# Loads in order of use, column scores ahead of the second tile's first layer, and matmuls that nothing reads, in a two-layer perceiver kernel

## The chip, the cores and the metric

The kernel runs on one core of a Trainium2 chip. A core has five engines that run beside each other, each in its own program order: TensorE (PE: matmuls, with weight loads shown as PEld), VectorE (DVE), ScalarE (ACT), GpSimd (POOL) and SyncE (SP, which here only issues transfers). Transfers run on 16 DMA engines. The metric is the device time of one execution in microseconds, as the median of several runs.

## What is computed

The reference adds six blocks to a stream x of 32 batches with 64 rows of 256 numbers each; a context of 32 batches with 1601 rows of 256 numbers is read by two of them.

```python
x = x + _L0_xattn_ref(_layernorm(x), ctx_1024, W, b)        # [x, mean of the context] @ W.T + b
x = x + _L0_attn_ref(_layernorm(x), ..., slopes)            # 16 heads over the 64 rows, with a slope by distance
x = x + _L0_ffn_ref(_layernorm(x), ...)                     # shared gated MLP, and 2 of 8 routed experts
x = x + _L1_xattn_ref(_layernorm(x), ctx_1024, ...)         # 16 heads of x over the 1601 context rows
x = x + _L1_attn_ref(_layernorm(x), ...)                    # causal convolution, gated recurrence, gated MLP
x = x + _L1_ffn_ref(_layernorm(x), w1, w2)                  # MLP with ternary weights and quantised rows
```

The order matters for what follows: a row of x goes through layer 0 (the first three lines) before its query exists, the query is needed for every score against the context, and layer 1's rest (the last two lines) comes behind that attention.

## The kernel before

**Tiles.** Two batches make a tile of 128 rows, 16 tiles in all. They are taken in the order 1, 2, ..., 15, 0 (`order`), so "pos 0" is the first tile taken and "pos 15" the last. All of it is float32, but for the ternary weights of the last MLP and some small bfloat16 helpers.

**The full stage.** Most of the time goes to the attention over the context. Each tile is cut into `NU` = 13 units (12 pieces of 512 context rows for one half of the heads of one batch, and one unit for the last 65 rows). The loop over `g` (13 x 16 units) does for each unit: `column_scores` (scores with the context on the partitions, L765 and L771, and their exponentials), `values` four units ahead, `row_scores` five units ahead (scores with the rows on the partitions, L723, from which VectorE takes the maxima, L730), `weighted` (the sums over the context, L795) and `keys` six units ahead. The maxima of a half of a tile must be known before its column scores: `maxima` splits their negative into three bfloat16 parts (L736 to L741), `maxima_rows` transposes these, and `column_scores` puts them into the score buffer first.

**The small chains.** Everything else of a tile is a generator that yields wherever it waits for another engine: `layer0` (a layer norm, the mixing with the context mean (`xat`), a second norm, the attention over 64 rows (`k`, `q`, `v`, `s`, a softmax on VectorE and ScalarE, the transposes `tpp`, the head sums `o`, the output `wo`), a third norm and the gated MLP (`su`, `sv`, `th`, the gate `lg`, `so`)); `query` (a norm `d`, a transpose `tp_d`, `q`, and `qbd` on VectorE); `tail` for the last two blocks, which is `recurrent` (norm `e`, transposes `tp_e`, `tp_f`, `tp_g`, the matmuls `pw`, `hg`, `gru`, `ff`, `ffo`) and then `bit_ffn` (the quantising helper `quantised` with its transposes `tpq`, and the matmuls `h`). `Steps` objects in a list `plan` advance these generators at two places of each unit, by due times in sixteenths of a tile. The four compute engines run in the order in which the code is recorded (`manual_schedule`); the order of SP's transfers is set by the framework from priorities and dependencies.

**Before the full stage.** `first` runs layer 0 and the query of pos 0 with nothing else to hide behind, and with it go keys and values of the first pieces (`early`), `early_sums` (context means of pos 1 to 3: four pieces each through the single buffer `part`, loaded by SP at L95 and summed by ScalarE at L243) and, as `beside`, layer 0 of pos 1. Then five row score groups, and what is left of `beside` is run to its end (`beside.all()`) before unit 0.

**The end.** After the last unit `tail` of pos 14 and `tail` of pos 15 are advanced in turn, the latter alone at the end.

**Buffers.** PSUM has three small buffers (`mm_tile`), two of two banks each for scores (`sc_tile`) and one for the weighted sums. A new tile in a buffer waits until the tile before in it has been read. Weights are loaded by `load_w` (L159), from POOL's queue where no engine is named; the rest of layer 1's weights follow from POOL too (L1027 to L1044).

## Time and profile before

| what | time |
|---|---|
| runs before (three) | 2213.13, 2213.56, 2221.24 us; median 2213.56 |
| the profiled execution | 2218.25 us, of which its span is 2216.6 |
| granted TensorE clock, mean over the span | 0.969 |
| PE busy | 2077.8 us (94%) |
| DVE busy | 1342.1 us (61%) |
| ACT busy | 909.1 us (41%) |
| POOL busy | 330.2 us (15%) |

"Span" is the time from the first to the last instruction of the profiled execution. The granted clock is the share of its full speed that TensorE was given; 0.50 in a stretch means that matmuls take twice as long there. In a timeline a line has the start, the duration, the engine, the line of the kernel, the operation, what it writes and reads, the shape and the count; what stands in square brackets is how long the engine had been idle before it and what ended that. In a table by stretches the columns are the stretch, its length, then for PE, PEld, DVE, ACT and POOL the busy time and the number of instructions, the granted clock, the busy share of the DMA engines and the GB/s that they moved.

### The profile page before, as it was taken

To read this page: it belongs to the slowest core of one execution; us is meant where nothing else is said; L and a number is where in the kernel's file an instruction comes from. 1 tells how busy PE (TensorE), PEld (TensorE's weight loads), DVE (VectorE), ACT (ScalarE), POOL (GpSimd) and SP (SyncE) were. 2 spreads that over 40 slices of the span, in tenths; PEclk is the share of its full clock that TensorE was granted. 3 is DMA by queue.
4 is the path that set the end of the run, shared out by engine and by line. 5 is a ranking of instruction groups with operands and counts; after the bars stand their busy time and mean duration, and the time that the engine had idled before them with its cause. 6 is when DMAs were issued, how large, how long until landed. Compare 5 with 4: busy or idle time off the path is not lost. (4 is left out here: it accounts for less than half of the span.)

```text
span 2216.6 us, 69786 instructions
## 1 busy us (share of the span) xinstructions
PE 2077.8 (94%) x31887; PEld 1520.4 (69%) x31903; DVE 1342.1 (61%) x2686; ACT 909.1 (41%) x1397; POOL 330.2 (15%) x545
## 2 busy tenths in 40 slices
PE   5799999999999999999999999999999899999984
PEld 3476777767676777777777677777776566676763
DVE  3446756665656666665666656565667656656554
ACT  3334444444535354444444435353433233334342
POOL 4211211111111121112111111111100000000011
PEclk8699999999999999999999999999999899999996
DMA  7423211111112121111211111110100200011000
GB/s 235 134 92 108 71 64 64 36 65 64 66 61 69 61 66 34 64 66 63 67 64 55 72 34 69 61 37 32 44 34 4 72 32 23 16 41 34 2 5 5
DMA packets 43463, 126.41 MB, mean 57 GB/s; under 512 B 11922, under 2 KB 25250, under 8 KB 43168
## 3 DMA queue, kind: packets, MB, share of 16 engines
q1 hardware_dynamic: 41312, 117.16, 15.8%
q8 instruction: 250, 4.10, 0.8%
q0 software_dynamic: 1296, 3.97, 0.5%
q10 hardware_dynamic: 560, 0.81, 0.1%
q14 instruction: 45, 0.37, 0.1%
HBM read 119.83 MB, written 2.10 MB: 55 GB/s over the span
## 5 line engine op out<-in xcount | busy, mean ns | idle before, releaser
L777 ACT ACTIVATE pt<-s 128x1024 f32<-128x1024 f32 (+1 forms) x416 | 403.5, 1022 | 299.0 <-PE s L771 298.9
L730 DVE TENSOR_REDUCE mx<-r 128x2 f32<-128x1024 f32 x384 | 452.1, 1220 | 114.8 <-PE r L723 114.5
L231 PE MATMUL vps<-w_L_xattn_WvT,ctxT 128*128 128x128 f32 x3072 | 398.9, 284 | 0.0
L231 PE MATMUL kps<-ctxT,w_L_xattn_WkT 128*128 128x512 f32 x768 | 383.9, 623 | 10.4 <-DMA ctxT<-ctxT 10.4
L690 ACT ACTIVATE kt<-kps,chv 128x512 f32<-128x512 f32 x192 | 132.2, 689 | 634.1 <-PE kps L231 634.1
L707 DVE COPY vau<-vps 128x512 f32<-128x512 f32 (+1 forms) x208 | 143.3, 689 | 390.3 <-PE vps L231 390.3
L231 PEld LDWEIGHTS vps<-w_L_xattn_WvT,ctxT 128*128 128x128 f32 x3072 | 362.7, 194 | 23.8 <-issue 3.1
L795 PEld LDWEIGHTS o<-pt,vau 128*32 128x32 f32 (+1 forms) x13312 | 196.5, 110 | 150.1 <-issue 143.3
L795 PE MATMUL o<-pt,vau 128*32 128x64 f32 (+1 forms) x13312 | 231.1, 221 | 4.2 <-ACT pt L777 4.2
L723 PE MATMUL r<-kt,qbd 32*128 32x512 f32 x1536 | 226.2, 649 | 1.4 <-DVE mx L727 0.8
L231 PEld LDWEIGHTS kps<-ctxT,w_L_xattn_WkT 128*128 128x128 f32 x768 | 131.7, 191 | 122.4 <-issue 105.3
L771 PEld LDWEIGHTS s<-qbd,kt 32*128 32x128 f32 x6144 | 207.2, 188 | 3.2
L771 PE MATMUL s<-qbd,kt 32*128 32x128 f32 x6144 | 207.7, 271 | 0.0
L243 ACT ACTIVATE part<-part 128x1601 f32<-128x1601 f32 x60 | 92.7, 1545 | 9.9 <-DMA part<-ctxT 9.6
L723 PEld LDWEIGHTS r<-kt,qbd 32*128 32x128 f32 x1536 | 62.9, 184 | 36.0 <-issue 18.4
L765 PEld LDWEIGHTS <-onesb 3*128 3x128 bf16 x768 | 21.0, 91 | 94.8 <-issue 93.5
L765 PE MATMUL s<-neg,onesb 3*128 3x512 bf16 x768 | 79.6, 386 | 6.9 <-DVE mx L730 6.7
L813 DVE RECIPROCAL rs<-sums 128x128 f32<-128x128 f32 x64 | 60.7, 948 | 1.7 <-PE sums L810 1.7
L309 POOL TENSOR_TENSOR kbd<-kT,mask 128x512 f32<-128x512 f32 x32 | 32.9, 1050 | 137.6 <-ACT kT L302 137.6
L231 PE MATMUL ff<-nT,w_fg 128*128 128x128 f32 x384 | 51.6, 287 | 1.0 <-ACT nT L925 1.0
L231 PEld LDWEIGHTS ff<-nT,w_fg 128*128 128x128 f32 x384 | 47.8, 200 | 1.9 <-ACT nT L925 1.7
L231 PE MATMUL ff<-nT,w_fv 128*128 128x128 f32 x384 | 48.3, 276 | 0.0
(352 smaller groups left out, 2562.7 us busy)
## 6 DMA issues: line engine op xcount, KB each, us to landing
ctxT<-ctxT SPq DMA_DIRECT2D x32, 1601.0 KB, 6.8
part<-ctxT SPq DMA_DIRECT2D x60, 800.5 KB, 4.5
rest<-ctxT SPq DMA_DIRECT2D x32, 65.0 KB, 2.2
x<-x SPq DMA_DIRECT2D x16, 128.0 KB, 2.2
out<-x SPq DMA_DIRECT2D x16, 128.0 KB, 1.7
w<-w SPq DMA_DIRECT2D x16, 128.0 KB, 2.4
sum_L_ffn_w1T<-L_ffn_w1T SPq DMA_DIRECT2D x4, 256.0 KB, 4.3
raw_L_ffn_w1T<-L_ffn_w1T SPq DMA_DIRECT2D x4, 256.0 KB, 3.1
```

The source lines that it names most:

```text
L231: nc.tensor.matmul(o, lhsT=lhsT(c), rhs=rhs(c), start=(c == 0), stop=(c == 1))
L243: nc.scalar.activation(junk, src, AF.Copy, accum_out=csum[:, c, b:b + 1])
L309: nc.gpsimd.tensor_tensor(kbd[oc], kT[:, oc, :].rearrange("p (b k) -> p b k", b=2).unsqueeze(2).to_broadcast([P, 2, 4, S]), mask4.unsqueez ...
L690: nc.scalar.activation(kt, o, AF.Identity, bias=chv[:, hf.oc, BK2:BK2 + 1])
L707: nc.vector.tensor_copy(v[:kr, :, 0:VW - 16].rearrange("p k (h d) -> p k h d", d=17)[:, :, :, 0:16], o[:kr].rearrange("p k (h d) -> p k h ...
L723: nc.tensor.matmul(o, lhsT=qbd[r, q % 2, q // 2].rearrange("p h q -> p (h q)"), rhs=w.kt[r, q, :] if h is None else halves[h].kt[k][r, :], ...
L730: nc.vector.tensor_reduce(w.mx[:, 2 * m:2 * m + 2, h % 4, k], ps[m], AX.X, ALU.max)
L765: nc.tensor.matmul(o, lhsT=onesb[r, :], rhs=halves[h].neg[r, :].unsqueeze(1).to_broadcast([3, 4, P]), start=True, stop=False)
L771: nc.tensor.matmul(ps[i // 2][:kr, i % 2, j * P:(j + 1) * P], lhsT=w.kt[r, j, :] if h is None else halves[h].kt[k][r, j * P:(j + 1) * P], ...
L777: nc.scalar.activation(pt[:kr].rearrange("p i k c -> p i (k c)"), ps[m][:kr], AF.Exp)
L795: nc.tensor.matmul(w.o[32 * c:32 * c + 32, q, m, :], lhsT=v[:kr, j, 17 * hd:17 * hd + 32], rhs=pts[m][:kr, c // 2, j, c % 2 * S:c % 2 * S ...
L813: nc.vector.reciprocal(rs, t)
```

## The change

It has three parts.

*Loads.* x of the first tile is loaded second, before the context (`early_x`). `load_w` uses SP's queue by default. The weights of the mixing stand ahead of the second context piece, the last 65 rows behind it; the other weights of layer 0 follow on SP. The weights of layer 1 that came from POOL are issued on SP by `late_weights`, at the step at which the context sums of pos 1 are complete in the program.

*Order.* Of the two calls of `others()` beside each row score group one goes, and `beside.all()` goes: what is left of pos 1's layer 0 is put into the plan for units 0 to 3. The query of pos 1 is due from 4 instead of 1, the ternary weights from 5 to 23 instead of 0 to 21.

*Matmuls that nothing reads.* `warm(n)` takes a score buffer and records n bfloat16 matmuls (128x128 by 128x512) into it; no instruction reads the result. It is called in `layer0` and `query` of the first tile (5, 22, 11, 6 and 11), before each of the first four row score groups (5 each), and in `recurrent` and `quantised` of the last tile (11, 18, 11, 18 and 18).

```diff
     def load_w(name, cols, chunks=2, eng=None):
-        (eng or nc.gpsimd).dma_start(t, a[name].rearrange("(c p) o -> p c o", p=P))
+        (eng or nc.sync).dma_start(t, a[name].rearrange("(c p) o -> p c o", p=P))
...
+    early_x = {}
+
+    def warm(n):
+        t = sc_tile("warm")
+        for _ in range(n):
+            nc.tensor.matmul(t[:, 0, :], lhsT=identb, rhs=onesb.unsqueeze(1).to_broadcast([P, 4, P]),
+                             start=True, stop=True)
...
-        x = load_x(ti)
+        x = early_x.pop(ti) if ti in early_x else load_x(ti)
...
+        if soon:
+            warm(5)
         xT = transposed(xn, f"b{ti}", SECOND["xT"] if k else "xT")
...
         def weights(oc):
+            if soon and oc == 0:
+                warm(22)
...
+        if soon:
+            warm(11)
         xT = transposed(xn, f"c{ti}", SECOND["xT"] if k else "xT")
...
+        if soon:
+            warm(6)
         o = mm_tile([P, D], f"so_{ti}")
...
-    def query(pos, x):
+    def query(pos, x, soon=False):
...
+        if soon:
+            warm(11)
         xT = transposed(xn, f"d{ti}", "xTq")
...
-    def recurrent(ti, x):
+    def recurrent(ti, x, soon):
...
+        if soon:
+            warm(11)
         t = transposed_ps(xs, f"f{ti}")
...
+        if soon:
+            warm(18)
         o = mm_tile([P, D], f"gru_{ti}")
...
+        if soon:
+            warm(11)
         t = transposed_ps(xs, f"g{ti}")
...
-    def quantised(v, n, tmp, sw, name):
+    def quantised(v, n, tmp, sw, name, soon):
...
+        if soon:
+            warm(18)
         t = mm_tile([P, 8, P], f"tpq_{name}", BF16)
...
-    w_k2 = load_w("L1_xattn_WkT", D, eng=nc.sync)
+    w_k2 = load_w("L1_xattn_WkT", D)
+    early_x[order[0]] = load_x(order[0])
     load_batch(0)
+    w_v2 = load_w("L1_xattn_WvT", D, eng=nc.scalar)
+    w_xat = load_w("L0_xattn_WT", D, 4)
+    load_batch(1)
     wholes[0].rest = load_rest(order[0])
-    w_v2 = load_w("L1_xattn_WvT", D, eng=nc.scalar)
-    load_batch(1)
-    w_xat = load_w("L0_xattn_WT", D, 4, nc.sync)
...
+    def late_weights():
+        for j in range(4):
+            nc.sync.dma_start(w_o2[32 * j:32 * j + 16], ...)
+            nc.sync.dma_start(bv2[32 * j:32 * j + 16], a["bv2"][j])
+        nc.sync.dma_start(w_pw, ...)
+        nc.sync.dma_start(w_hg, ...)
+        nc.sync.dma_start(w_go[:DI], ...)
+        for w, name in ((w_fg, "L1_attn_w_gate"), (w_fv, "L1_attn_w_value")):
+            nc.sync.dma_start(w[:, :, :FF], a[name].rearrange("(c p) f -> p c f", p=P))
+        nc.sync.dma_start(w_fo[:, 0:NF - 1, :], ...)
+        nc.sync.dma_start(w_fo[0:FF - last, NF - 1, :], ...)
...
     def second_layer(pos):
-        yield from tail(order[pos], x4[pos])
+        yield from tail(order[pos], x4[pos], pos == NT - 1)
...
         if pos < NT - 1:
-            planned(queried(pos), 16 * (pos - 1) + 1, 16 * (pos - 1) + 8.5, 6, 0)
+            planned(queried(pos), 16 * (pos - 1) + (1 if pos > 1 else 4), 16 * (pos - 1) + 8.5, 6, 0)
...
+        late = [late_weights]
         while 0 not in queries:
             if early:
                 early.pop(0)()
             ahead.step()
             others()
-        for f in early:
+            if 1 in csums and late:
+                late.pop()()
+        for f in early + late:
             f()
         for g in range(4):
+            warm(5)
             row_scores(g)
             others()
-            others()
         maxima(0)
         row_scores(4)
         others()
         maxima_rows(0)
-        beside.all()
+        if beside.gen is not None:
+            plan.insert(0, Steps(beside.gen, 0, 3, 30 - beside.done, 2))
...
-        planned(all_ternary(), 0, 21, 24, 2)
+        planned(all_ternary(), 5, 23, 24, 2)
```

More of the change, by code (lines that the diff above doesn't have):

```diff
@@ L968, in quantised, with bit_ffn @@
         return qT, d
-    def bit_ffn(ti, x):
+    def bit_ffn(ti, x, soon):
         m = moments(x, f"h{ti}")
@@ L974, in bit_ffn @@
         tmp = work_tile([P, D], "xs", f"qt_{ti}")
-        qT, d = yield from quantised(n, D, tmp, sw1, f"h{ti}")
+        qT, d = yield from quantised(n, D, tmp, sw1, f"h{ti}", soon)
         yield ACT
@@ L982, in bit_ffn @@
         yield
-        qT, d = yield from quantised(h, HID, h, sw2, f"i{ti}")
+        qT, d = yield from quantised(h, HID, h, sw2, f"i{ti}", soon)
         yield
@@ L990, in bit_ffn, with tail @@
         nc.sync.dma_start(out[ti * P:(ti + 1) * P, :], x6)
-    def tail(ti, x):
-        x = yield from recurrent(ti, x)
-        yield from bit_ffn(ti, x)
+    def tail(ti, x, soon):
+        x = yield from recurrent(ti, x, soon)
+        yield from bit_ffn(ti, x, soon)
     order = list(range(1, NT)) + [0]
@@ L1005, in load_batch @@
         ctxs[n] = load_ctx(2 * hf.ti + hf.b)
-    w_k2 = load_w("L1_xattn_WkT", D, eng=nc.sync)
+    w_k2 = load_w("L1_xattn_WkT", D)
+    early_x[order[0]] = load_x(order[0])
     load_batch(0)
+    w_v2 = load_w("L1_xattn_WvT", D, eng=nc.scalar)
+    w_xat = load_w("L0_xattn_WT", D, 4)
+    load_batch(1)
     wholes[0].rest = load_rest(order[0])
-    w_v2 = load_w("L1_xattn_WvT", D, eng=nc.scalar)
-    load_batch(1)
-    w_xat = load_w("L0_xattn_WT", D, 4, nc.sync)
-    w_k = load_w("L0_attn_WkT", D, eng=nc.sync)
-    w_q = load_w("L0_attn_WqT", D, eng=nc.sync)
-    w_v = load_w("L0_attn_WvT", D, eng=nc.sync)
-    w_o = load_w("L0_attn_WoT", D, eng=nc.sync)
-    w_gate = load_w("L0_ffn_w_gateT", E)
+    w_k = load_w("L0_attn_WkT", D)
+    w_q = load_w("L0_attn_WqT", D)
+    w_v = load_w("L0_attn_WvT", D)
+    w_o = load_w("L0_attn_WoT", D)
     w_s1 = load_w("L0_ffn_sw1T", D)
     w_s3 = load_w("L0_ffn_sw3T", D)
+    w_gate = load_w("L0_ffn_w_gateT", E)
     w_s2 = load_w("L0_ffn_sw2T", D)
@@ L1026, in perceiver_kernel @@
     nc.gpsimd.memset(bv2, 0.0)
-    for j in range(4):
-        nc.gpsimd.dma_start(w_o2[32 * j:32 * j + 16], a["L1_xattn_WoT"].rearrange("(g j d) o -> j d g o", j=4, d=16)[j])
-        nc.gpsimd.dma_start(bv2[32 * j:32 * j + 16], a["bv2"][j])
-    w_pw = load_w("L1_attn_pw_wT", D)
+    w_pw = const.tile([P, 2, D], F32, name="w_pw")
     w_hg = const.tile([P, 2, 2 * DI], F32, name="w_hg")
-    nc.gpsimd.dma_start(w_hg, a["L1_attn_w_hg"].rearrange("(c h) d e -> (h d) c e", c=2))
     w_go = const.tile([P, 4, 64], F32, name="w_go")
     nc.gpsimd.memset(w_go[DI:], 0.0)
-    nc.gpsimd.dma_start(w_go[:DI], a["L1_attn_w_out"].rearrange("h e o -> e h o"))
     w_fg = const.tile([P, 2, NF * P], F32, name="w_fg")
     w_fv = const.tile([P, 2, NF * P], F32, name="w_fv")
-    for w, name in ((w_fg, "L1_attn_w_gate"), (w_fv, "L1_attn_w_value")):
+    for w in (w_fg, w_fv):
         nc.gpsimd.memset(w[:, :, FF:], 0.0)
-        nc.gpsimd.dma_start(w[:, :, :FF], a[name].rearrange("(c p) f -> p c f", p=P))
     w_fo = const.tile([P, NF, D], F32, name="w_fo")
     nc.gpsimd.memset(w_fo[:, NF - 1, :], 0.0)
-    nc.gpsimd.dma_start(w_fo[:, 0:NF - 1, :], a["L1_attn_w_ff_out"][0:(NF - 1) * P, :].rearrange("(f p) o -> p f o", p=P))
-    nc.gpsimd.dma_start(w_fo[0:FF - (NF - 1) * P, NF - 1, :], a["L1_attn_w_ff_out"][(NF - 1) * P:FF, :])
+    def late_weights():
+        for j in range(4):
+            nc.sync.dma_start(w_o2[32 * j:32 * j + 16],
+                              a["L1_xattn_WoT"].rearrange("(g j d) o -> j d g o", j=4, d=16)[j])
+            nc.sync.dma_start(bv2[32 * j:32 * j + 16], a["bv2"][j])
+        nc.sync.dma_start(w_pw, a["L1_attn_pw_wT"].rearrange("(c p) o -> p c o", p=P))
+        nc.sync.dma_start(w_hg, a["L1_attn_w_hg"].rearrange("(c h) d e -> (h d) c e", c=2))
+        nc.sync.dma_start(w_go[:DI], a["L1_attn_w_out"].rearrange("h e o -> e h o"))
+        for w, name in ((w_fg, "L1_attn_w_gate"), (w_fv, "L1_attn_w_value")):
+            nc.sync.dma_start(w[:, :, :FF], a[name].rearrange("(c p) f -> p c f", p=P))
+        last = (NF - 1) * P
+        nc.sync.dma_start(w_fo[:, 0:NF - 1, :], a["L1_attn_w_ff_out"][0:last, :].rearrange("(f p) o -> p f o", p=P))
+        nc.sync.dma_start(w_fo[0:FF - last, NF - 1, :], a["L1_attn_w_ff_out"][last:FF, :])
     def ternary(name, chunks, cols):
@@ L1168, in first @@
         x3[0] = yield from steps
-        yield from query(0, x3[0])
+        yield from query(0, x3[0], True)
     def biased():
```

## The prediction

> **What bounds it now.** I read the page's slices first, then busy time in three stages, then the timeline of the first 120 us and of the last 60.

> ```profile
> PE   5799999999999999999999999999999899999984
> PEclk8699999999999999999999999999999899999996
> ```
> ```profile
> 0.00:118.50 118.50, 75.08 (x431) 51.82 (x432) 47.25 (x95) 35.72 (x60) 36.05 (x72) 0.74 0.54 174
> 118.50:2120.00 2001.50, 1945.73 (x30713) 1424.04 (x30726) 1248.45 (x2485) 845.20 (x1284) 278.37 (x445) 0.99 0.16 53
> 2120.00:2216.60 96.60, 56.95 (x751) 44.53 (x751) 46.40 (x107) 28.17 (x53) 15.83 (x28) 0.77 0.02 5
> ```
> The second row's PE is busy 97% at clock 0.99: what the change puts into that stage costs its full TensorE time. All that can be won lies in the first and third rows (clock 0.74 and 0.77), where one tile's chain runs from engine to engine. The first stage in order:

> ```profile
> 28.04 0.43 DVE L187 BATCH_NORM_STATS2 st_a<-x 128x6 f32<-128x256 f32 x1 [17.28 <-DMA x<-x]
> ...
> 34.55 1.40 PE L280 MATMUL xat<-w_L_xattn_WT,xT_a 128*128 128x256 f32 x4
> ...
> 66.53 0.36 ACT L235 ACTIVATE th<-su 128x256 f32<-128x256 f32 x1
> ...
> 84.59 1.12 DVE L662 SCALAR_TENSOR_TENSOR qbd<-q,chv,mask2q 128x128 f32<-128x128 f32 x4 [2.57 <-PE q L231]
> ...
> 118.49 0.61 PE L765 MATMUL s<-neg,onesb 3*128 3x512 bf16 x4
> ```
> The first tile's x arrives only at 28.0; its queries (qbd) are done at 85.7; the first column scores start at 118.49. The clock, microsecond by microsecond:

> ```profile
> 76.00:77.00 1.00, 0.61 (x2) 0.29 (x2) 0.85 (x3) 0.00 (x0) 0.21 (x2) 0.62 0.62 256
> ...
> 83.00:84.00 1.00, 1.00 (x13) 0.83 (x10) 0.00 (x0) 0.99 (x3) 0.00 (x0) 0.96 0.00 0
> ```
> It falls to half at about 76.2, 2.0 us after a matmul group ended at 74.2, and returns at 83.0, 5.4 us after TensorE became busy again at 77.6. Elsewhere: it fell 4.4 us after 47.9, 3.1 us after 2162.1; it rose 4.6 us after 30.7, 4 us after 2184.8, and only 8.5 us after 64.35. So waits of 2 to 4.4 us lose it; 4 to 8.5 us of work bring it back.

> **The change, part by part.** *Price of one idle matmul.* The nearest rows are the 128x512 bf16 matmuls of the last MLP: three in 0.81 us at full clock (each 0.38 long, so one starts every 0.215) and two in 1.06 at half clock (0.63 long, one every 0.43). A group of 11 is 2.4 or 4.7 us, 18 is 3.9 or 7.7.

> *First loads.* x now stands second on SP's queue, ahead of the first context piece: 0.13 MB at the 346 GB/s of 10:20 put that piece, and the keys that wait for it at 10.4, 0.4 us later. The second piece (landed 20.5, 2.81 + 17.7) gets w_xat ahead of it (0.52 MB, 1.5 us), but POOL's weights, 1.4 MB by then, are out of its way (4 us): about 18, and no sum waits for it. POOL loses its transfers; its fills end near 8 and its next work is behind x's statistics, so that is worth nothing. In the built program each SP transfer waits for the one eight places earlier; that binds only the small weights behind the second piece, whose first reader (k) comes at 32. With x there, the next wait is the column sums: ScalarE's second sum ended at 22.2 (20.61 + 1.54), set by the keys before it, and mT can follow at 22.5 instead of 34.51: 12.0 earlier. Two blocks of values (2.0 each) and five idle matmuls (1.1) now stand ahead of tp_b, which moves from 40.2 to about 30.1. The softmax wait of 5.8 us before tpp takes 22 idle matmuls (4.7) without delay; at full clock tpp, wo and tp_c save 1.0 + 1.0 + 0.3, so xT_c comes at 51.5 instead of 63.9.

> What is late next: ScalarE sums the next tiles' context pieces in program order, and the fifth sum stands ahead of th. There is one "part" buffer: the piece is issued when the last is summed, lands 4.5 us later (median of 60), is summed in 1.74, with 0.15 for the issue: 6.4. Five from 22.4 are 54.4; the third also waits 2.1 for the two exponentials ahead of it: 56.5. So th stands at 57.0, not at 53: **-9.5**. The late weights (2.9 MB, formerly POOL's queue) now lie between those pieces on SP; I leave the landing at 4.5, since DMA was busy 24% in 50:60, but see the second rival.

> *th to qbd.* 18.1 us before. lg needs the buffer that th reads, so TensorE waits 3.0 (54.4 to 57.4) and I take the clock as lost (2.0 lost it above). It returns near the end of xat; then xat saves 0.5, k, q and v run at 1.05 + 1.06 + 1.09 instead of 2.08 + 1.70 + 1.73: 2.8 in all with the rounding of the rise. The 6 idle matmuls lie beside VectorE's chain from xat to tp_b (3.1), the 11 ahead of tp_d have no cover, since tp_d followed q at once: 2.4 lost. Sum about **-0.9**: qbd ends at 75.3.

> *First column scores ahead of the second tile.* From the end of qbd to column scores the trace has 32.8. What stays is VectorE's: 1.29 for s, 1.31, 1.21, four times 2.36, 1.47, 1.05 of maxima, 0.2, together 16.0; ahead of it s_2 and one idle group on TensorE (2.2, beside the 1.29). The idle tile also takes one of the two score buffers, so a row group now waits for both reductions of the last one instead of the first: 0.7 in three places; half-clock row groups cost 1.05 instead of 0.5 each. I take 21 (20 to 24): **-11.8**; column scores at 96.3.

> The rest of the second tile then runs inside units 0 to 2 of the full stage. At full-clock rows: tpp 1.04, o 0.86, wo 1.08, tp_c 0.4, su and sv 2.1, lg 0.5, so 1.03: 7.0. TensorE keeps program order, so three waits stand in front of the row scores and weighted sums queued behind them: pT between the two o groups (1.0 to 1.4), wo to tp_c (60.53 to 63.20: 2.7), the buffer of tp_a (0.3). The clock is half at the start, for 3 to 5 us against 1.1 before: 1.7. Sum **+13.0** (11 to 16). Query and ternary steps that move by units add no TensorE work: 0, bounds -2 to +2 by the 2.5 us of VectorE waits at 180 to 183.

> *The last tile.*

> ```profile
> 2166.19 0.39 PE L965 MATMUL tpq_h<-identb,q_h 128*128 128x128 bf16 x2 [4.06 <-POOL q_h L960]
> ...
> 2168.73 0.64 PE L215 MATMUL tp_f<-ident,xs_f 128*128 128x128 f32 x2
> ...
> 2178.56 1.89 PE L987 MATMUL h<-wq_L_ffn_w2T,qT_i 128*128 128x256 bf16 x8 [1.16 <-DVE zz L904]
> 2180.24 1.81 PE L912 MATMUL gru<-w_go,rr 128*128 128x64 f32 x8
> ```
> In the built order the first 11 stand between h and tp_f, and 18 between h and gru. Neither has a wait there: tp_f and gru follow the work of the tile before at once. Both meet a half clock (waits of 4.06 and 4.36 just before). I take 3.9 (2.4 to 4.7) and 5.6 (3.9 to 7.7). hg gives back 0.9, gru 0.8, tp_g 0.25, ff 1.6 (4.63 to 3.0). The groups of 11 and 18 after that fit the waits of 2.8, 4.9 and 5.3, and the last MLP at full clock saves 0.1 + 0.65 + 0.4 + 0.85. So 9.5 - 5.5 = **+4.0** (+1 to +7).

> **Sum.** -9.5 - 0.9 - 11.8 + 13.0 + 4.0 = -5.2 on the profiled execution (2218.25, span 2216.6). The median of the runs shown is 4.7 lower, 2213.56; from there 2208.4.

> [...]

> **Rivals.** *The clock holds.* If it survives the 3.0 us before lg, lg, xat and so run full: qbd 3 us earlier still; the row groups take 20, units 0 to 2 cost 11, the tail 2.5: -12.4 - 12.8 + 11 + 2.5 = -11.7, 2202. For: at 83.0 to 87.9 it survived waits of 0.7 and 0.8. Against: 76.2. Chance 0.22.

> *Pieces land late, and it is slower.* ScalarE's in-order sums wait for SP's queue, where weights now stand ahead of each piece. The first piece before, behind such weights, took 9.2 (issued 23.06, awaited until 32.4 at most). At 9.2 for all five, th is at 22.4 + 5 x 11.1 = 77.9, 21 later than forecast: 2229. The gain is gone when they land in (5.2 + 2.1)/5 = 1.5 more than 4.5: from 6 us it isn't faster. For: 2.9 MB in 30 us. Against: those weights are issued while the piece before is still being summed. Chance 0.13.

> *The idle matmuls don't lift the clock.* Then the tail pays 4.7 + 7.7 and overruns of 1.9, 2.8 and 2.4: +19.5; the row phase is 24, qbd gains 6.4, units cost 13.5: -6.4 - 8.8 + 13.5 + 19.5 = +17.8, 2231. Against: 2189.0, where dense work did lift it. Chance 0.05.

> **Numbers.** Forecast 0.60, 2208.4, own range 2203 to 2214. A measurement of this kernel can tell about 0.5% from no change: below 2202.5 or above 2224.6. Faster: four fifths of the first rival and a twelfth of the forecast, 0.22. Slower: two fifths of the second and most of the third, 0.08. The rest 0.70. The range 2199 to 2217 leaves out about 0.06 below and 0.12 above.

> **What would show it.** x's statistics near 5 us; th near 57 with a ScalarE wait for "part" ahead of it; qbd near 74, column scores near 96; TensorE waits before tp_c in unit 1; gru 4 us or more after the end of h, where it followed h at once; the last MLP's 128x512 matmuls 0.215 apart. Wrong if th follows xT_c without a wait, if units 0 to 2 show no TensorE waits, or if the tail is shorter than 96 us.

## The result, and the profile after

| | median | lowest to highest | runs |
|---|---|---|---|
| before | 2217.84 us | 2213.13 to 2221.24 | 6 |
| after | 2208.02 us | 2206.75 to 2214.36 | 6 |

The ratio of after to before is 0.9967, with a 95% interval of 0.9952 to 0.9982: a gain of 0.33%, some 7.3 us (4.0 to 10.6); the two medians lie 9.8 apart. The profiled execution after took 2207.64 us, its span 2205.9, 10.7 less than the span before.

The slices of the page after, PE's busy tenths and the granted clock, each digit a fortieth of the span:

```profile
PE   7799999999999999999999999999999899999976
PEclk9999999999999999999999999999999899999998
```

Only the first two digits and the last ones differ from before. The table by stretches of the kernel after (columns as before: PE, PEld, DVE, ACT, POOL, clock, DMA share, GB/s):

```profile
0.00:118.50 118.50, 88.01 (x737) 55.13 (x738) 55.83 (x104) 39.83 (x65) 24.59 (x55) 0.94 0.54 181
118.50:2120.00 2001.50, 1943.01 (x30819) 1424.30 (x30835) 1248.40 (x2493) 849.34 (x1296) 278.05 (x447) 0.99 0.15 52
2120.00:2205.90 85.90, 59.17 (x496) 39.95 (x490) 39.18 (x91) 18.09 (x37) 12.70 (x24) 0.88 0.01 4
```

In the first stretch the clock went from 0.74 to 0.94 and PE is busy 13 us more, with idle matmuls and with the first units, which begin in it now. The middle is what it was. The first stage in the timeline of after:

```profile
5.83 0.43 DVE L197 BATCH_NORM_STATS2 st_a<-x 128x6 f32<-128x256 f32 x1 [1.71 <-DMA x<-x]
...
24.64 1.03 PE L290 MATMUL xat<-w_L_xattn_WT,xT_a 128*128 128x256 f32 x4
...
56.35 1.54 ACT L253 ACTIVATE part<-part 128x1601 f32<-128x1601 f32 x1 [1.85 <-DMA part<-ctxT]
...
57.88 0.36 ACT L245 ACTIVATE th<-su 128x256 f32<-128x256 f32 x1
...
58.56 0.61 PE L241 MATMUL lg<-w_L_ffn_w_gateT,xT_c 128*128 128x8 f32 x4 [1.75 <-ACT xT_a L231]
...
72.22 1.13 DVE L682 SCALAR_TENSOR_TENSOR qbd<-q,chv,mask2q 128x128 f32<-128x128 f32 x4 [4.10 <-PE q L241]
...
95.33 0.62 PE L785 MATMUL s<-neg,onesb 3*128 3x512 bf16 x4 [2.09 <-DVE neg L768]
...
106.73 0.43 PE L397 MATMUL o<-pT,vbd 128*32 128x64 f32 x16 [0.96 <-ACT pT L390]
...
113.93 0.41 PE L225 MATMUL tp_c<-ident,xn_c 128*128 128x128 f32 x2 [2.70 <-DVE xn_c L207]
```

x is there 22 us sooner, xat starts 9.9 sooner, and the chain then meets the context pieces: th stands behind a piece that ScalarE awaits 1.85 us. qbd is 12.4 and the column scores are 23.2 earlier. The same column scores of unit 3 start at 130.68 instead of 143.49, only 12.8 earlier: the rest of the second tile's layer 0 lies in units 0 to 2 now, with two waits of TensorE, 0.96 ahead of o and 2.70 ahead of tp_c. The last tile:

```profile
2155.85 3.45 PE L190 MATMUL warm<-onesb,identb 128*128 128x512 bf16 x11
2159.14 0.38 PE L225 MATMUL tp_f<-ident,xs_f 128*128 128x128 f32 x2
...
2167.75 1.89 PE L1015 MATMUL h<-wq_L_ffn_w2T,qT_i 128*128 128x256 bf16 x8 [1.16 <-ACT qT_i L995]
2169.43 5.00 PE L190 MATMUL warm<-onesb,identb 128*128 128x512 bf16 x18
2174.27 1.00 PE L936 MATMUL gru<-w_go,rr 128*128 128x64 f32 x8
```

tp_f and gru show no wait: each followed at once on idle matmuls, which stood in the queue where before the transpose and gru themselves stood.

### The profile page after: what moved, and what is told of

Read it like the earlier page. It is cut to its first block, busy times and chain, and to the rows that moved or that the text cites. A ratio compares the mean times of both kernels' runs of the same rounds, so it can differ in the third digit from the quotient of the medians.

```text
span 2205.9 us, 70071 instructions
## 1 busy us (share of the span) xinstructions
PE 2090.2 (95%) x32038; PEld 1519.4 (69%) x32054; DVE 1343.4 (61%) x2686; ACT 907.3 (41%) x1397; POOL 315.3 (14%) x525
## 5 line engine op out<-in xcount | busy, mean ns | idle before, releaser
L253 ACT ACTIVATE part<-part 128x1601 f32<-128x1601 f32 x60 | 92.6, 1544 | 17.5 <-DMA part<-ctxT 17.3
L241 PE MATMUL ff<-nT,w_fv 128*128 128x128 f32 x384 | 49.4, 280 | 0.0
```

The lines of the kernel that those rows point to most:

```text
L241: nc.tensor.matmul(o, lhsT=lhsT(c), rhs=rhs(c), start=(c == 0), stop=(c == 1))
L253: nc.scalar.activation(junk, src, AF.Copy, accum_out=csum[:, c, b:b + 1])
```

## The experiments

Each kernel was run beside the kernel before, whose medians there were 2216.02 to 2218.30; the ratio is to that. Dates come from one profiled execution each, which for "order only" and "without the 11 before tp_d" was the slowest of that kernel's runs; the columns th, column scores and unit 3 are starts as well; the last column is from the start of the last `pw` to the end of the span.

| kernel | median, us | ratio (95%) | th | qbd starts | column scores | unit 3 | last pw to the end |
|---|---|---|---|---|---|---|---|
| before | 2217.84 | 1 | 66.53 | 84.59 | 118.49 | 143.49 | 55.5 |
| after | 2208.02 | 0.9967 (0.9952 to 0.9982) | 57.88 | 72.22 | 95.33 | 130.68 | 57.5 |
| no idle matmuls | 2209.17 | 0.9963 (0.9948 to 0.9977) | 56.22 | 74.35 | 94.41 | 131.97 | 55.5 |
| loads only | 2209.98 | 0.9974 (0.9964 to 0.9984) | 57.70 | 73.69 | 104.96 | 131.03 | 55.5 |
| order only | 2214.33 | 0.9990 (0.9978 to 1.0001) | 67.09 | 85.23 | 106.50 | 144.93 | 55.6 |
| late weights on POOL | 2216.85 | 1.0001 (0.9993 to 1.0010) | 64.15 | 78.48 | 101.60 | 139.29 | 57.3 |
| sums first | 2208.02 | 0.9962 (0.9949 to 0.9975) | 55.29 | 69.63 | 92.75 | 128.00 | 57.5 |
| without the 11 before tp_d | 2211.06 | 0.9970 (0.9960 to 0.9981) | 57.50 | 69.47 | 93.05 | 130.58 | 59.1 |
| row groups' in the mm ring | 2209.77 | 0.9965 (0.9952 to 0.9979) | 57.84 | 72.18 | 92.87 | 130.93 | 57.5 |
| spread over units 0 to 5 | 2212.20 | 0.9976 (0.9966 to 0.9986) | 57.34 | 71.68 | 94.80 | 128.20 | 58.6 |
| tail without two groups | 2203.98 | 0.9948 (0.9933 to 0.9963) | 57.33 | 71.68 | 94.79 | 133.00 | 52.7 |
| tail covered | 2201.49 | 0.9939 (0.9922 to 0.9956) | 57.58 | 71.93 | 95.05 | 130.22 | 51.3 |
| combined | 2201.22 | 0.9927 (0.9914 to 0.9941) | 55.25 | 70.94 | 91.62 | 129.52 | 49.4 |
| last | 2196.85 | 0.9903 (0.9886 to 0.9919) | 53.97 | 66.36 | 86.74 | 124.30 | 53.2 |

### The three parts alone

**No idle matmuls**, loads and order as changed:

```diff
     def warm(n):
-        t = sc_tile("warm")
-        for _ in range(n):
...
+        return
```

> The changed kernel without any of its idle matmuls; loads and order stay. My account (the loads carry the gain, the idle matmuls about pay for themselves): th 58 to 60.5 instead of 57.9, since tpp, wo and tp_c run at half clock again; row reductions 3.06 apart instead of 3.75, since the idle tile no longer takes a score buffer; from pw to the end of the span 55.5, as before the change, instead of 57.5; in all 2205 to 2209, the changed kernel's time within 2. Rival (the idle matmuls are what lifts the clock and carry the gain): no clock in the row phase and the tail, 8 to 12 us lost, about 2217.

The time is that of after: all 14 groups together are worth nothing that can be measured. The trace shows gains and losses that about cancel: without them th to qbd takes 18.1 instead of 14.3, but qbd to the column scores 20.1 instead of 23.1, and the tail 55.5 instead of 57.5. Two lines of VectorE's timeline without them:

```profile
78.92 2.35 DVE L746 TENSOR_REDUCE mx<-r 128x2 f32<-128x1024 f32 x2
82.32 2.36 DVE L746 TENSOR_REDUCE mx<-r 128x2 f32<-128x1024 f32 x2 [1.05 <-PE r L739]
```

The reductions are 3.40 apart, not 3.06 as expected: row groups at half clock (the eight matmuls at 87.00 took 3.21, as those of before at 91.64 with the clock at 0.50) leave a gap of 1.05. With the idle matmuls they are 3.75 apart. That th came earlier without them (56.22) was not expected either: the first context piece was issued 1.35 us sooner there (22.89 instead of 24.24), and th stands behind the fifth.

**Loads only**: as above, and the order of before (both calls of `others()`, `beside.all()`, the old due times).

> The first loads of the changed kernel, with the order of steps and the absence of idle matmuls of the kernel before. My account (the loads are the gain, the order gives nothing net): th 58 to 60.5, qbd ends at 76 to 78, the first column scores 32.8 later, 109 to 111, that is 8 to 10 ahead of before, and this lead is kept: 2208 to 2210. Rival (the order carries the gain; the second tile's layer 0 eats an early start): column scores at 115 or later, 2215 to 2218.

The time is as expected. The column scores came 4 sooner than expected, and the lead over before at unit 3, 12.5, is almost that of after (12.8); at the last pw 8.4 are left of it.

**Order only**, on the kernel before:

```diff
             row_scores(g)
             others()
-            others()
...
-        beside.all()
+        if beside.gen is not None:
+            plan.insert(0, Steps(beside.gen, 0, 3, 30 - beside.done, 2))
...
-        planned(all_ternary(), 0, 21, 24, 2)
+        planned(all_ternary(), 5, 23, 24, 2)
```

> The kernel before with only the order of steps changed (column scores ahead of the rest of the second tile's layer 0, query and ternary steps moved). My account: the 10.8 that the changed kernel gains from qbd to the column scores come back as 10.3 in units 0 to 2, so 2216 to 2218, no change. Rival (the order is the gain): 5 or more faster, 2213 or less.

PE's first matmuls of the column scores, units 0 to 3:

```profile
106.50 0.61 PE L765 MATMUL s<-neg,onesb 3*128 3x512 bf16 x4 [2.09 <-DVE neg L748]
118.45 0.39 PE L765 MATMUL s<-neg,onesb 3*128 3x512 bf16 x4
134.94 0.40 PE L765 MATMUL s<-neg,onesb 3*128 3x512 bf16 x4
144.93 0.40 PE L765 MATMUL s<-neg,onesb 3*128 3x512 bf16 x4
```

The first comes 12.0 earlier than before, the fourth 1.4 later: what the order wins it gives back. The median, 2214.33, lies 1.7 below the range of my account; the interval of the ratio, 0.9978 to 1.0001, leaves room for a gain of up to 4.9 us, just short of the rival's 5.

### Which of the loads

**Late weights on POOL's queue**, at the start, as before the change; x stays early:

```diff
-            nc.sync.dma_start(w_o2[32 * j:32 * j + 16],
+            nc.gpsimd.dma_start(w_o2[32 * j:32 * j + 16],
...
+    late_weights()
...
-        late = [late_weights]
+        late = []
```

> The changed kernel with the late weights issued on POOL's queue at the start, as before the change, instead of on SP's between the context pieces. My account (they cost each piece 0.5 to 0.9 of its landing, and the fifth piece 1.8 of ScalarE's wait ahead of th): pieces land in 4.5 instead of 4.9 to 5.3, th at 56.2, where the chain through su holds it, instead of 57.9; the second whole context piece lands later (its sum at 18 to 21 instead of 16.96), which may move mT by up to 2 and eat that. Rival (pieces land late whatever shares the queue): th at 57.5 or later.

My account was wrong, and by more than its rival's bound: the whole gain in the median is gone (1.0001). ScalarE's timeline, then one line of VectorE's:

```profile
26.04 0.37 ACT L231 COPY xT_a<-tp_a 128x256 f32<-128x256 f32 x1 [1.29 <-PE tp_a L225]
36.76 1.54 ACT L253 ACTIVATE part<-part 128x1601 f32<-128x1601 f32 x1 [10.36 <-DMA part<-ctxT]
```
```profile
21.41 0.82 DVE L207 TENSOR_SCALAR xn_a<-x,mv_a,rstd_a 128x256 f32<-128x256 f32 x1 [13.55 <-POOL rstd_a L202]
```

The first piece, issued at 27.70, landed 9.06 later, with DMA at 356 GB/s from 20 to 30; in after it was issued at 24.24 and took 4.94, with DMA at 187 GB/s. So its sum started 7.6 later, and th 6.3 later. The second piece landed in 4.80 again.

A second effect stood in neither account. POOL issued the late weights from 7.78 to 20.40, ahead of rstd_a in its program order. VectorE waited 13.55 us for rstd_a, both context sums ran from 22.14 (in after they started at 11.48 and 16.96), and mT came at 26.43, 2.2 later. That chain doesn't set th here: ScalarE still awaits the fifth piece, for 0.95, just ahead of it.

So what counts in the first loads is that layer 1's weights aren't issued before the first sums are done (from 25.1 in after). With x early and those weights where they were, the trace is 4.2 ahead of before at unit 3, the last tile then takes 1.8 more, and the median gains nothing. The converse, the weights moved and x left where it was, was not run.

**Sums first**: the sums of each whole piece are recorded as soon as it has landed, ahead of the keys' copies.

```diff
+        for _ in range(3):
+            next(steps)
+        both(0)
+        yield
+        both(1)
+        csums[0] = csum
...
-        for b in range(2):
-            yield
-            summed(order[0], csum, b, 0, ctxs[b][:, 0, :], junk)
```

> The changed kernel with the first tile's context sums emitted as soon as each piece lands (ScalarE: ahead of the first keys copy and of the second), so that mT no longer waits for the keys. My account (th is set by five context pieces in a row from the end of the first sums, and by a chain that starts at mT): mT at 18.8 to 19.5 instead of 24.24, th at 52.5 to 53.5 instead of 57.9, column scores at 90 to 91, all of it kept: 4 to 5 faster. Rival (the pieces then compete with the second whole context piece and the weights, and land late): th at 56 or later, no gain.

```profile
18.53 0.29 DVE L284 TENSOR_SCALAR mT<-csum 128x256 f32<-128x256 f32 x1
```
```profile
25.86 1.54 ACT L253 ACTIVATE part<-part 128x1601 f32<-128x1601 f32 x1 [6.13 <-DMA part<-ctxT]
...
53.75 1.54 ACT L253 ACTIVATE part<-part 128x1601 f32<-128x1601 f32 x1 [1.44 <-DMA part<-ctxT]
55.29 0.36 ACT L245 ACTIVATE th<-su 128x256 f32<-128x256 f32 x1
```

mT (VectorE's line) came 5.7 earlier, th (ScalarE's) only 2.6: the first piece, issued at 18.72, took 7.14 to land instead of 4.94, which is part of the rival's account. Neither account had th right (52.5 to 53.5, or 56 and later). th still follows the fifth piece. The 2.6 reach unit 3 (128.00), but the time is that of after; with runs from 2203.5 to 2215.8 a gain of this size can't be told.

### Idle matmuls without cover, in the first stage

**Without the 11 before tp_d:**

```diff
-        if soon:
-            warm(11)
         xT = transposed(xn, f"d{ti}", "xTq")
```

> The changed kernel without the 11 idle matmuls ahead of tp_d alone. My account (they have no cover and the clock is already full there): tp_d follows q at 67.5, qbd starts at 70.0 instead of 72.2, and th to qbd's start shrinks from 14.3 to 12.1; column scores 2 earlier. Rival (they are what carries the clock over the waits to qbd and the first row groups): th to qbd stays at 14 or the row phase from qbd grows from 23.1 to 25.

qbd started at 69.47, 2.75 earlier, th to qbd 12.0: they had no cover, and the clock held without them up to qbd (the eight matmuls of q ahead of it took 1.16 in both). The column scores came 2.3 earlier, unit 3 only 0.1: in this profile the clock fell in units 0 to 2 (0.54 from 112 to 115), in that of after it didn't (1.00 from 110 to 119). The time didn't follow (the last section comes back to both).

**The row groups' five in another ring**, so that they hold no score buffer:

```diff
-        t = sc_tile("warm")
+        t = mm_tile([P, 512], "warm_r") if row else sc_tile("warm")[:, 0, :]
```

> The changed kernel with the five idle matmuls ahead of each row group in a buffer of the mm ring instead of one of the two score buffers. My account (the idle tile holds a score buffer, so a group waits for both reductions of the last): row reductions 3.0 to 3.1 apart instead of 3.75, column scores 2.2 earlier after the end of qbd (19.8 instead of 22.0). Rival (TensorE's own five idle matmuls and four row matmuls set the 3.75): still 3.75 apart and 22.0.

```profile
78.35 4.80 DVE L748 TENSOR_REDUCE mx<-r 128x2 f32<-128x1024 f32 x4
84.17 2.36 DVE L748 TENSOR_REDUCE mx<-r 128x2 f32<-128x1024 f32 x2 [1.02 <-PE r L741]
```

The four reductions of two groups ran without a gap, one gap of 1.02 stayed; from the start of qbd the column scores take 20.7 instead of 23.1, as expected. The score buffer was the cause. Unit 3 starts no sooner (130.93), since here too the clock fell in units 0 to 2 (0.66 from 112 to 115), and again the time stays.

**The second tile spread over units 0 to 5:**

```diff
-            plan.insert(0, Steps(beside.gen, 0, 3, 30 - beside.done, 2))
+            plan.insert(0, Steps(beside.gen, 0, 5, 30 - beside.done, 2))
...
-(1 if pos > 1 else 4)
+(1 if pos > 1 else 6.5)
```

> The changed kernel with the rest of the second tile's layer 0 spread over units 0 to 5 instead of 0 to 2 (its query steps 2.5 sixteenths later). My account (in units 0 to 2 TensorE waits for a chain whose steps stand too close together: 0.96 for pT, 2.70 for xn_c): with more work between the steps both waits go, and the column scores of unit 7 come 3 to 4 after those of unit 0 less than now (73.1). Rival (the waits come from VectorE and ScalarE being behind, whatever the distance): they move to units 3 to 5 and 73.1 stays within 1.

```profile
111.25 0.70 PE L241 MATMUL wo<-w_L_attn_WoT,oT 128*128 128x256 f32 x2 [0.90 <-ACT oT L400]
120.12 1.16 PE L241 MATMUL su<-xT_c,w_L_ffn_sw1T 128*128 128x128 f32 x8 [0.46 <-ACT xT_c L231]
165.76 0.69 PE L225 MATMUL tp_d<-ident,xn_d 128*128 128x128 f32 x2 [5.53 <-DVE xn_d L207]
```

In place of the waits of 0.96 and 2.70 there are now 0.90 ahead of wo and 0.46 ahead of su, but the chain now ends so late that its query isn't ready for the row scores of the second tile: 5.53 in one place. Unit 7 starts 76.9 after unit 0, not 73.1. Neither account had this wait.

### The tail

**Without the 11 before tp_f and the 18 before gru:**

```diff
-            warm(11)
+            pass
         t = transposed_ps(xs, f"f{ti}")
...
-            warm(18)
+            pass
         o = mm_tile([P, D], f"gru_{ti}")
```

> The changed kernel without the 11 idle matmuls before tp_f and the 18 before gru. My account (these two stand uncovered): 3.45 + 5.0 come out of the chain, hg and gru at half clock give back 0.9 + 0.8, the 11 before tp_g overrun their cover by 1.4 at half clock, ff loses 0.8: pw to the end 53 instead of 57.5, 2203.5. Rival (the clock they lift is worth as much in the rest of the tail): pw to the end 57 to 59, 2207.5 to 2209.5.

As my account had it: 52.7 from pw to the end, 4.9 less than after, and 2203.98. The two groups had taken 8.5, so what they gave back was 3.6.

**And 18 in each wait of the last tile but one:**

```diff
-        yield from bit_ffn(ti, x, soon)
+        yield from bit_ffn(ti, x, ti in order[-2:])
```

> The kernel without the two uncovered groups of the tail, and 18 idle matmuls instead in each of the last tile but one's two waits (4.06 ahead of tpq_h, 4.36 ahead of tpq_i). My account (only idle matmuls inside a wait pay): the clock holds over h, tp_f, hg, h, gru, which save 0.4 + 0.25 + 0.9 + 0.8 + 0.8, and the 11 ahead of tp_g end 1.2 sooner: pw to the end 49 to 50 instead of 52.7, 3 faster than without the cover. Rival (the chain through VectorE's scan sets gru, not TensorE's queue): 51 to 52.

```profile
2146.62 4.05 PE L190 MATMUL warm<-onesb,identb 128*128 128x512 bf16 x18
2150.84 0.29 PE L993 MATMUL tpq_h<-identb,q_h 128*128 128x128 bf16 x2 [0.18 <-POOL q_h L986]
...
2161.73 1.05 PE L1015 MATMUL h<-wq_L_ffn_w2T,qT_i 128*128 128x256 bf16 x8 [1.16 <-ACT qT_i L995]
2163.62 1.72 PE L936 MATMUL gru<-w_go,rr 128*128 128x64 f32 x8 [0.84 <-DVE rr L929]
```

Both groups fit their waits (0.18 left) and h ran at full clock (eight matmuls in 1.05, 1.89 in after), but gru now waits 0.84 for VectorE's scan: the rival's reason. From pw to the end it takes 51.3, only 1.3 less than without the cover, where my account had 3.

### Put together

**Combined**: sums first, the row groups' matmuls in the mm ring, the covered tail, and 7 idle matmuls in the 1.61 us wait ahead of tp_g of the last tile but one.

> All that helped: sums as the pieces land, the row groups' idle matmuls in the mm ring, the tail without its two uncovered groups and with 18 in each wait of the last tile but one, and 7 in the wait of 1.61 ahead of its tp_g. My account (front gains are kept one to one): th 55.3, column scores at 90.2, pw to the end 51.4, 2196 to 2199. Rival (units 0 to 2 and the phase of the clock take the front's part back): 2200 to 2203.

2201.22: the rival's number, not that of my account. The column scores came at 91.62, 3.7 before those of after; unit 3 only 1.2 before.

**Last**: the combined kernel without the 11 before tp_d, and with the fifth sum behind th:

```diff
-            if 0 in csums:
+            if 0 in csums and not held:
                 summing.step()
...
+        if soon:
+            held.append(ti)
         yield ACT
         u_ps = mm_tile([P, 2, P], f"su_{ti}")
...
+        held.clear()
         g_ps = mm_tile([P, E], f"lg_{ti}")
```

> The combined kernel without the 11 idle matmuls ahead of tp_d, and with the fifth context sum put behind th and the next tile's xT_a on ScalarE. My account (the fifth piece alone held th by about 2; the 11 held qbd by 2.3): th at 53.3 to 53.8 right behind su instead of 55.3, th to qbd 12.0 instead of 15.7, column scores at 86 to 88, 3 to 5 faster than combined: 2196 to 2198. Rival (the front's last microseconds are taken back in units 0 to 2 and by the phase of the clock): column scores at 88 or earlier but the time within 1 of combined, 2200 to 2202.

```profile
53.97 0.38 ACT L244 ACTIVATE th<-su 128x256 f32<-128x256 f32 x1 [1.25 <-PE su L240]
55.08 0.37 ACT L230 COPY xT_a<-tp_a 128x256 f32<-128x256 f32 x1 [0.73 <-PE tp_a L224]
55.35 1.54 ACT L252 ACTIVATE part<-part 128x1601 f32<-128x1601 f32 x1
```

th now waits for su, not for a piece, which shows that the fifth piece had held it. 2196.85 us, ratio 0.9903: about 0.64% less than the kernel after (0.9903 / 0.9967, two ratios from separate runs).

## Why the prediction was right, and where its sizes were off

2208.4 was forecast and 2208.02 measured. That they agree to 0.4 us is luck: the sum of -5.2 was laid on 2213.56, the median of three runs, and six runs give 2217.84, from where it would give 2212.6, above five of the six runs after. The sum itself lies inside the interval of -4.0 to -10.6, and is half of what the two traces show. Term by term, from the two profiled executions:

| term | forecast | measured | from |
|---|---|---|---|
| to th | -9.5 | -8.65 | 66.53 to 57.88 |
| th to qbd | -0.9 | -3.72 | 18.06 to 14.34 |
| qbd to the column scores | -11.8 | -10.79 | 33.90 to 23.11 |
| units 0 to 2 | +13.0 | +10.35 | 25.00 to 35.35 |
| unit 3 to the last pw | 0 | +0.08 | 2017.61 to 2017.69 |
| last pw to the end | +4.0 | +2.0 | 55.5 to 57.5 |
| sum | -5.2 | -10.7 | |

- **To th.** The mechanism held: five pieces in a row, with ScalarE's wait ahead of th. They landed in 4.94, 5.22, 4.55 and 5.01 where the trace shows it, against 4.5. mT came at 24.24, not 22.5, since the keys started 1.2 later and ran at half clock until about 17.5 (their weight loads are 0.85 apart until then and 0.43 behind it; the clock column reads 1.00 there). The forecast's own pieces end at 56.5; the 0.5 from there to its 57.0 has no reason. The second rival's price of 9.2 is what the first piece costs when the late weights stay where they were (9.06); moving them is what prevented it. The forecast had the number and didn't see that it was the main gain.
- **th to qbd.** This step failed in size: "I take the clock as lost". xT_c came at 54.12, not at 51.5, so TensorE waited 1.75 ahead of lg, not 3.0, and it waited for the copy xT_a, which follows th on ScalarE. The clock stayed full (1.00 from 51.7 to 89.2), as the first rival said for this place. The 11 before tp_d had no cover, as forecast: without them qbd is 2.75 earlier. The forecast's terms, 2.8 saved and 2.4 lost, give -0.4, not -0.9; this slip and the 0.5 of th cancel in the sum.
- **qbd to the column scores.** 22.0 from qbd's end instead of 21; gaps of 1.39 between the reductions where 0.7 was forecast. The reason, the score buffer, is shown by the ring experiment.
- **Units 0 to 2.** The waits were 0.96 and 2.70, as forecast. The sum of 13.0 is right for most of the profiled executions: in eleven with this order (all but the spread one), units 0 to 2 took 37.5 to 38.4 in eight (12.5 to 13.4 over before) and 35.2 to 35.4 in three, of which the profiled one of after is one. The difference is a fall of the clock at the wait of 2.70, which the last section shows. With the usual 38 the traces would give -8, close to the ratio's 7.3.
- **Unit 3 to the last pw.** That this stretch is the same to 0.08 in the two profiles is chance too: in those eleven it took 2015.5 to 2024.7.
- **Tail.** The two uncovered groups cost 3.45 + 5.0 = 8.5 (forecast 9.5), and the clock that all five groups of the last tile lift gave back 6.4 (forecast 5.5). Taking the two out won 4.9 of the tail. The table's last row after, 85.9, begins later in the program than that of before; from the same place the tail takes 98.6 instead of 96.6, so the sign "shorter than 96 us" did not occur.
- **Rivals.** Idle matmuls did lift the clock (0.88 in the tail instead of 0.77), so the third falls. The first rival's terms (-12.4 to qbd, -12.8, +11, +2.5, in all -11.7) are nearer to this pair of profiles (-12.4, -10.8, +10.4, +2.0) than the forecast's, but for the row groups. Its condition, a wait of 3.0 that the clock survives, wasn't met, and its 11 for units 0 to 2 holds in three profiles of eleven.

## What to carry to other kernels

At a start that is bound by transfers, ask first which bytes needn't move yet, and which engine is held up by issuing them: here 2.9 MB of late weights decided, and x, order and idle matmuls without that were together worth nothing in the median (ratio 1.0001). An idle matmul paid here only inside a wait that it didn't outlast (the two groups of the tail without one took 8.5 and gave back 3.6), and its output tile is a buffer like any other (as a score buffer it left gaps of 1.39 between the reductions). Work that was moved from a bare chain into a stage whose engine is full came back at its full price: 10.8 won ahead of the column scores, 10.4 given back in units 0 to 2.

## What the runs showed of the hardware

A wait's length alone didn't decide whether the clock fell. PE by half microseconds (busy, clock, DMA share, GB/s), after and then the kernel with the covered tail, around the same wait of 1.61 ahead of tp_g:

```profile
2133.50:2134.00 0.50, 0.20 (x1) 0.80 0.00 0
2134.00:2134.50 0.50, 0.46 (x2) 0.50 0.00 0
...
2140.50:2141.00 0.50, 0.00 (x0) 0.87 0.00 0
```
```profile
2133.50:2134.00 0.50, 0.05 (x1) 1.00 0.00 0
...
2135.00:2135.50 0.50, 0.50 (x5) 1.00 0.00 0
```

And around the wait of 2.70 ahead of tp_c, in after and in the kernel without two groups of the tail, which has the same first stage:

```profile
113.50:114.00 0.50, 0.07 (x1) 1.00 1.01 423
...
115.00:115.50 0.50, 0.50 (x16) 1.00 1.04 435
```
```profile
115.00:115.50 0.50, 0.50 (x5) 0.65 1.01 423
...
118.50:119.00 0.50, 0.50 (x13) 0.94 1.00 399
```

In each pair the instructions and the wait are the same, and the clock fell in one and not in the other. The wait of 2.70 is in all eleven profiles with this order: in three the clock stayed at 1.00 behind it, in eight it fell, and those are the three with 35.2 to 35.4 in units 0 to 2 and the eight with 37.5 and more. (In that of order only the fall is read from the matmuls: the eight of `r` behind tp_c took 2.09, those at the end of unit 2 1.14.) From the shares within the half microseconds, after fell at 2133.80 and rose at 2140.63, 6.83 later; the other fell at 115.15 and rose at 118.56, 3.41 later: two times and one time the same step. The second fall came when TensorE had been busy again for 0.5. In six more of the eight, what the stretches behind the wait lost makes 3.4 us at half clock as well (without idle matmuls 0.60 from 113 to 116 and 0.83 from 116 to 119, so 3.42).

What went with a fall was how busy TensorE was within a step. Behind the first 20 us of before and after, all 16 steps at full clock with at most 41% ended in a fall, 7 of the 56 with 45 to 77% did, and none of the 1154 above. Where the clock stayed at the wait of 2.70 in after, the wait was split over two steps (busy 45 and 76%); in the kernel without two groups of the tail it lay in the one that ended with the fall at 115.15 (busy 21%). At the wait of 1.61 it was 36% in after. Why steps between 45 and 77% went either way is open.

Such falls are also the likely reason why front gains of 2 to 3 us didn't show in the medians: a fall in units 0 to 2 cost 2.9 (38.2 against 35.35 in the second pair), the stretch behind them differs by up to 9 between the eleven profiles, and runs of one kernel differ by up to 12. The tail isn't spared: the last kernel's, the same program as the combined kernel's, took 53.2 instead of 49.4, with hg in 2.02 (at 2150.72) and gru in 1.94 (at 2160.78) where the other's took 1.16 and 1.08.

The clock isn't all of it. In the profile of the kernel without the 11 before tp_d it was 0.85 from 560 to 564 and 0.73 from 564 to 568, where after had no fall (1.00 in both stretches), and behind it the same matmuls were 3.4 later against after than ahead of it. Ahead of that fall TensorE stood still in the middle of 32 matmuls:

```profile
562.35 0.45 PE L789 MATMUL s<-qbd,ktr 32*65 32x128 f32 x7 [1.51 <-issue]
```

The profile names nothing that it waited for. After has no such stop of more than 0.3 in the full stage; those without idle matmuls and with order only have one too, of 1.12 (at 438.15) and 1.18 (at 450.97), all three within the 32 matmuls of a tile's last 65 rows, and the cause is open. Why the medians of the kernels with one front edit show none of their gain, and the last kernel's does, is not settled either: a single profile of each can't tell how often its clock falls.
